# Tile 105 by rows, the first types one group later, the second block's steps six tiles later

## Chip, cores and metric

The kernel runs on one core of a Trainium2 chip. The metric is the device time of one execution in microseconds (us): the median over the runs of a kernel.

## What is computed

A graph layer with relations: 12,500 nodes with 256 features, 212,500 edges that are sorted by their end (`dst`), and a type of 8 for each edge. `h` is the normalised and rectified `x`. Each edge sends its source's `h` through the weight of its type; a node sums what comes in, and adds a bias, its own `h` through a loop weight, and `x`.

```python
h   = maximum(layernorm(x), 0)                # 12500 x 256
hx  = einsum('ni,rio->rno', h, weight)        # 8 types
msg = hx[edge_type, src]                      # 212500 x 256
agg = segment_sum(msg, dst, num_segments=12500)
out = x + sqrt(0.5) * agg + h_bias + sqrt(0.5) * (h @ loop_weight)
```

## The kernel before

**Turned about.** The kernel sums the `h` rows of the edges by (end node, type) first and multiplies by the weights afterwards. The sums stand in a ring in SBUF (`acc`, 768 columns of nodes for each of 8 types and two halves of features).

**Tiles and units.** The edges are cut into 1578 tiles, two to a unit. One tile is at most 128 source rows, fetched into a buffer `msg` (one row to a partition). `edge_sums(t)` (line 1019) multiplies them on PE with one-hot columns that DVE makes (`onehots`, L1001), into one of four PSUM banks; `add_sums(u)` adds a unit's bank to the ring on DVE (L1072). The first units form block 0 (80 units, tiles 0 to 159), then come blocks of 128 units; for each block `prepare(b)` is a list of small steps, most of them on DVE, that work out its source indices (`gidx`), the columns of its one-hots, the last edge of each node and the places in the ring.

**Fetching rows.** Nearly every tile is fetched by one indirect transfer that POOL issues (`gather`, L944). The first 88 tiles take raw rows of `x` and are normalised in place; later ones take rows of `h`, which the kernel writes to DRAM in its first part (rows loaded and stored by SP, L894 and L900; normalisation is queued to the end at tile 28). A ring of 66 buffers holds tiles; `goal(t)` says how far gathers may run ahead: 64 tiles, from tile 170 on falling to 24, and less at the very end. Each gather also waits in the program for the unit last summed when it is issued.

**Single tiles by rows.** From tile 155 on, every 26th tile (155, 181, ..., 55 in all) is not gathered: `single_rows(t)` is true for it, and `begin_fetch` puts four pieces of 32 rows into queues of SP and ACT, two pieces each. A piece loads 32 offsets into registers (`load_sources`, L965) and issues 32 transfers of one row (L973, 1 KB). `fetch` takes up to four entries of each queue at each tile, from HOLD = 8 tiles after the tile would have been gathered. PE waits on a counter for the 128 rows (L1036) ahead of that tile's sums.

**Groups.** 98 groups of 128 nodes (the first has 84) follow in order: when a group's last unit is summed, its 18 products (L1252) are spread between the tiles' sums, then `finish(g)` adds bias and `x` and hands over the store. `finish(g)` also readies the ring's slot of group g + 6: for the first eight groups the slot is only cleared on ACT (`clear`); from group 8 on `begin(b)` writes each node's own edge into it, a transpose of its rows of `h` on PE and eight DVE operations (L1114). For that, the types of those own edges must be known, for four groups at a time (index q): `mark(q)` (DVE, L1135) and `find_types(q)` (a product on PE, L1145; comparisons on DVE, L1152 and L1157; a product that spreads them, L1164; a cast, L1168). The first q that needs this is `plan.typed` = 2, groups 8 to 11.

**One bank for odd jobs.** Transposes and products of this kind share the PSUM bank `pt`. `shared` queues such a job, `advance` starts the first one that is ready, and keeps ROOM = 5 tiles between them; where a product needs a result that is still queued, the queue is forced through in order (`advance(None)`).

**Order.** The program is written out by the Python loop `for t in range(NT)`; each engine then works through its own list in that order. Steps of a block have a due tile, start of the block's list + LOADED (EARLY for block 1) + number, and run about one a tile when a budget (`credit`) allows. Before, block 1's 46 steps start at tile 31 and end at tile 93; group 0 is finished at tile 55, group 1 at 69, group 2 at 87, group 3 at 103, group 4 at 121.

Of the kernel before, what the change touches and what calls it, by code (L numbers as in the profile page):

```python
# [20 lines left out]
SP = mybir.EngineType.SP  # L21
ACT = mybir.EngineType.Activation
# [6 lines left out]
XG = 4  # L29
# [12 lines left out]
NEAR = 8  # L42
# [13 lines left out]
AHEAD = 64  # L56
# [5 lines left out]
CLOSE = 8  # L62

SINGLE = 26
FETCH = 4
SOURCES = 32
BY_SP = (0, 2)
# [7 lines left out]
QUAD = 4  # L75
# [18 lines left out]
LATE = -4  # L94
# [1 line left out]

PREP = 232
LOADED = 20
EARLY = 30
HELD = 30  # L100
SETTLE = 4
ROOM = 5
# [149 lines left out]
def kernel(  # L252
# [20 lines left out]
    plan = Plan(N, E)  # L273

    NT = plan.NT
# [13 lines left out]
    h32 = dram.tile([N, D], F32, name="h32")  # L289
# [41 lines left out]
    with ExitStack() as main:  # L331
# [37 lines left out]
        state = {"h32": None}  # L369
# [439 lines left out]
        for d in range(0, N, XG * P):  # L809
            k = min(XG, (N - d) // P)  # L810
# [101 lines left out]

        def single_rows(t):

            return (t % SINGLE == SINGLE - 1 and t + 2 * NEAR < NT
                    and state["h32"] is not None and t // QUAD * QUAD >= state["h32"] + LATE + AHEAD)

        def begin_fetch(t):

            if t not in msg:  # L920
                room(t - t % PAIR)
            fetched[t] = len(fetched)
            for k, r in enumerate(range(0, P, SOURCES)):
                engine = SP if k in BY_SP else ACT
                fetches[engine].append((
                    done["tile"] + HOLD,
                    lambda r=r, engine=engine: load_sources(t, r, engine)))
# [177 lines left out]
        def begin(g):  # L1105

            s0, n = slot(g)
            q = g // XG
            o = plan.starts[g] - plan.starts[XG * q]
            turn, keep, pst = turn_nodes(g, selves)  # L1110

            def own(r):
                of = typed[q][:, o : o + n].unsqueeze(1).to_broadcast([P, KC, n])
                i = nc.vector.scalar_tensor_tensor(  # L1114
                    acc[:, :, r, s0 : s0 + n], of, float(r + 1), pst[:, :, :n],
                    op0=ALU.is_equal, op1=ALU.mult)
                in_run("own", i, r == R - 1)
                if r == R - 1:
                    zeroed[g, "slot"] = i.ins

            def write():
                for r in range(R):
                    writes.append((g, 0.42, lambda r=r: own(r)))

            shared(turn, [(2, write), (2, keep)], lambda: q in typed)
# [101 lines left out]
        def group_work(g):  # L1227

            d0 = plan.starts[g]
            s0, n = slot(g)  # L1230
            first_dep = [True]
            final = plan.NG - 1 if plan.NG > SLOTS + 1 else None

            def biased(g):
                q, k = divmod(g, XG)
                n = plan.ends[g] - plan.starts[g]
                rows_ = got["x", q]
                nc.vector.tensor_add(rows_[:n, k, :], rows_[:n, k, :], outs[g % 2][:n, 1, :])  # L1238

            def product(r, c, g=g):  # L1240
                n = plan.ends[g] - plan.starts[g]
                if (r, c) == (R, 0):
                    while g == final and final - 2 not in finished:
                        late.pop(0)[1]()
                    got["out", g] = outs[g % 2][:, 0, :]
                if r == R:
                    while ("self", g) not in got:
                        advance(None)
                    lhs, rhs = got["self", g][:, c, :n], wl[:, c, :]
                else:  # L1250
                    lhs, rhs = acc[:, c, r, s0 : s0 + n], w[:, c, r * D : (r + 1) * D]
                i = nc.tensor.matmul(got["out", g][:n], lhs, rhs, start=(r == R and c == 0),  # L1252
                                     stop=(r == R - 1 and c == KC - 1))
                latest["pe"] = in_run(
                    "loops" if r == R else "products", i, r >= R - 1 and c == KC - 1).ins
                if (r, c) == (R, 0) and g < 2:
                    tc.add_manual_dep(i.ins, done["bias"], SYNC_DEP, reason="one engine at a time")
                if r < R and first_dep[0]:
                    first_dep[0] = False
                    tc.add_manual_dep(i.ins, added[plan.last[g]].name, SYNC_DEP, reason="sums complete")  # L1260

            def finish():
                finished.add(g)
                q, k = divmod(g, XG)
                rows_ = got["x", q]
                if g != final:
                    biased(g)
                nc.vector.tensor_add(rows_[:n, k, :], rows_[:n, k, :], got["out", g][:n])  # L1268
                if final is not None and g != final and done["tile"] >= NT - HELD:
                    alone = rows_[:n, k, :]  # L1270
                    stores.append((NT, lambda: nc.sync.dma_start(out[d0 : d0 + n], alone)))
                elif XG * (q + 2) >= plan.NG or n < P:
                    nc.sync.dma_start(out[d0 : d0 + n], rows_[:n, k, :])
                elif k == XG - 1:
                    first = plan.starts[XG * q + shorts(q)]
                    to, of = out[first : d0 + n].rearrange("(k p) d -> p k d", p=P), rows_[:, shorts(q) :, :]
                    stores.append((done["tile"] + STORE, lambda: nc.sync.dma_start(to, of)))
                b = g + SLOTS
                q, k = divmod(b, XG)
                if b < plan.NG:  # L1280
                    if q < plan.typed:
                        clear(b)
                    else:
                        begin(b)
                if q + 1 >= plan.typed and XG * (q + 1) < plan.NG:
                    if k == max(XG // 4, SLOTS - XG * q):
                        load_groups("h", h32, q + 1)
                    if k == XG - 2 + (q + 1 == plan.typed):
                        mark(q + 1)
                    if k == XG - 1:  # L1290
                        find_types(q + 1)

            def last():
                done["late"].append((done["tile"] + REST, finish))

            work = []
            for r in [R, *range(R)] if g != final else range(R):
                for c in range(KC):
                    work.append((0.55, lambda r=r, c=c: product(r, c)))
            work.append((0.0, last))  # L1300
            if final is not None and g == final - 1:
                work = [(0.55, lambda c=c: product(R, c, final)) for c in range(KC)] + work
                work.append((0.0, lambda: biased(final)))
            return work
# [290 lines left out]
```

## Time and profile before

| | us |
|---|---|
| median of 3 runs | 1935.35 (1934.03 to 1936.07) |
| profiled execution | 1935.85 |
| span in that profile | 1934.1 |
| PE busy | 1683.9 (87%) |
| POOL busy | 1448.6 (75%) |
| DVE busy | 1313.7 (68%) |
| ACT busy | 132.0 (7%) |

The span runs from the first to the last instruction; the execution's own time has 1.75 us more. PE is TensorE, DVE VectorE, ACT ScalarE, POOL GpSimd, SP SyncE. An engine's busy time doesn't count the issuing of transfers by SP and ACT, register loads, or waits. A row of a timeline gives start, duration, engine, line, operation and tiles, and in brackets the idle time ahead of it with what ended it; SPq is SP issuing transfers.

### The profile page before, as it was taken

The page shows a single profiled execution, that of the slowest core. Times are in us where ns is not written, and L with a number is a line of the kernel's source. Part 1 is how long each engine was busy: PE and PEld are TensorE (multiplying, and loading weights), DVE is VectorE, ACT ScalarE, POOL GpSimd, SP SyncE. Part 2 cuts the span into 40 slices and gives each one's busy share as a digit, 9 for nine tenths or more (in the row PEclk, how much of TensorE's full clock was granted, in tenths as well). Part 3 has the DMA queues.
Part 4 walks back from the last instruction along what each step waited for, and adds up shares of the span by engine and source line. Part 5 has one row for each costly group of instructions (what it writes and reads, how often), then busy time and mean ns, then how long its engine had stood idle before and what let it go on. Part 6 is the DMA issues. An engine that isn't in the chain of part 4 may idle for free.

```text
span 1934.1 us, 41835 instructions
## 1 busy us (share of the span) xinstructions
PE 1683.9 (87%) x10152; PEld 1477.3 (76%) x10152; DVE 1313.7 (68%) x3304; ACT 132.0 (7%) x286; POOL 1448.6 (75%) x1549
## 2 busy tenths in 40 slices
PE   2367999998998898989898898989998898889998
PEld 2357889897897777878787776777777688777987
DVE  6878768975776865667776666776566685665662
ACT  6964000000000000000000000000000000000000
POOL 7777777777777777777777777777777777777774
PEclk9568999999999998998999999999999999999999
DMA  9974445544454444454444454444444445444443
GB/s 315 381 225 138 133 129 142 142 133 133 131 143 133 132 131 134 131 142 133 132 133 133 132 141 134 131 132 132 131 123 122 133 131 143 121 139 131 112 117 93
DMA packets 159789, 279.23 MB, mean 144 GB/s; under 512 B 36319, under 2 KB 110802, under 8 KB 159538
## 3 DMA queue, kind: packets, MB, share of 16 engines
q0 software_dynamic: 73104, 199.72, 36.6%
q1 hardware_dynamic: 77384, 73.17, 12.5%
q10 hardware_dynamic: 9050, 3.63, 1.1%
q8 instruction: 80, 1.31, 0.3%
q14 instruction: 171, 1.40, 0.2%
HBM read 250.78 MB, written 25.60 MB: 143 GB/s over the span
## 4 chain that ended last, share of the span: by engine, by line
PE 36%; DMA 29%; POOL 13%; issue 7%; DVE 6%; SPq 6%; ACT 2%; DVEq 0%; POOLq 0%; ACTq 0%; PEldq 0%
DMA msg<-h,gidx 26%; PE po L1252 18%; PE ps L1039 17%; POOL msg L944 13%; SPq L973 5%; DVE acc L1072 1%; SPq L965 1%; ACT msg L876 1%; DMA msg<-h 1%; DVE stats L832 1%; DMA xt<-in_x_dram 1%; DVE oh L1001 1%; DVE moves L458 1%; ACT xt L876 0%; DVE acc L1114 0%
## 5 line engine op out<-in xcount | busy, mean ns | idle before, releaser
L944 POOL DMA_INDIRECT msg<-h,gidx x1435 | 1362.6, 950 | 438.7 <-issue 368.2
L1039 PEld LDWEIGHTS ps<-oh,msg 128*128 128x128 f32 x6312 | 942.4, 199 | 349.0 <-DMA msg<-h,gidx 204.1
L1039 PE MATMUL ps<-oh,msg 128*128 128x136 f32 (+1 forms) x6312 | 995.6, 289 | 202.6 <-DMA msg<-h,gidx 121.4
L1252 PE MATMUL po<-w,acc 128*128 128x256 f32 (+1 forms) x3136 | 892.5, 390 | 2.0 <-DVE acc L1072 1.7
L1072 DVE TENSOR_TENSOR acc<-acc,ps 128x352 f32 x789 | 408.4, 518 | 372.3 <-PE ps L1039 364.4
L1252 PEld LDWEIGHTS po<-w,acc 128*128 128x128 f32 (+1 forms) x3136 | 521.8, 194 | 41.7 <-issue 12.4
L1114 DVE SCALAR_TENSOR_TENSOR acc<-types,pt 128x256 f32<-128x256 bf16 x720 | 259.7, 414 | 71.7 <-PE pt L1096 64.2
L1001 DVE TENSOR_TENSOR oh<-fixed,cols 128x544 f32<-128x544 f32 x395 | 282.8, 716 | 0.0
L1252 PE MATMUL po<-wl,self_t 128*128 128x256 f32 (+1 forms) x392 | 117.7, 427 | 8.5 <-DVE self_t L1101 6.1
L944 POOL DMA_INDIRECT msg<-in_x_dram,gidx x86 | 82.0, 953 | 26.9 <-issue 23.8
L1252 PEld LDWEIGHTS po<-wl,self_t 128*128 128x128 f32 (+1 forms) x392 | 74.6, 212 | 18.9 <-DVE self_t L1101 7.5
L1168 DVE CAST types<-pt 128x512 bf16<-128x512 f32 x23 | 15.9, 691 | 54.2 <-PE pt L1164 54.2
L1238 DVE TENSOR_TENSOR xr<-xr,po 128x256 f32<-128x256 f32 (+1 forms) x98 | 40.6, 414 | 15.8 <-PE po L1252 15.8
L1268 DVE TENSOR_TENSOR xr<-xr,po 128x256 f32<-128x256 f32 (+1 forms) x98 | 41.2, 421 | 10.6 <-PE po L1252 7.3
L876 ACT ACTIVATE msg<-msg,shift,rstd 128x256 f32<-128x256 f32 x88 | 44.8, 587 | 7.1 <-DVE stats L840 5.3
L1101 DVE COPY self_t<-pt 128x256 f32<-128x256 f32 (+1 forms) x98 | 40.8, 417 | 3.3 <-PE pt L1096 2.8
L458 DVE TENSOR_SCALAR moves<-fixed 128x271 int32<-128x271 int32 (+1 forms) x90 | 40.6, 451 | 3.4 <-DVE acc L1072 2.2
L1096 PE MATMUL pt<-ident,hr 128*128 128x128 f32 (+1 forms) x196 | 38.8, 281 | 2.2 <-DMA hr<-h 1.0
L460 DVE COPY_PREDICATED fixed<-moves,fixed 128x311 int32<-128x311 int32 (+14 forms) x90 | 38.0, 422 | 3.1
L876 ACT ACTIVATE xt<-xt,shift,rstd 128x256 f32<-128x256 f32 x66 | 33.7, 587 | 10.3 <-DVE shift L873 10.3
L1152 DVE TENSOR_TENSOR of<-pt,line 22x512 bf16<-22x512 f32 x23 | 15.7, 682 | 25.3 <-PE pt L1145 25.1
L1096 PEld LDWEIGHTS pt<-ident,hr 128*128 128x128 f32 (+1 forms) x196 | 25.7, 150 | 4.4 <-DVE types L1168 1.6
(167 smaller groups left out, 367.5 us busy)
## 6 DMA issues: line engine op xcount, KB each, us to landing
msg<-h SPq DMA_DIRECT2D x3520, 1.0 KB
msg<-h ACTq DMA_DIRECT2D x3520, 1.0 KB
msg<-h,gidx POOLq DMA_INDIRECT x1435
hr<-h SPq DMA_DIRECT2D x23, 512.0 KB
xr<-in_x_dram SPq DMA_DIRECT2D x23, 512.0 KB
out_dram<-xr SPq DMA_DIRECT2D x22, 512.0 KB
xt<-in_x_dram SPq DMA_DIRECT2D x16, 512.0 KB
h<-xt SPq DMA_DIRECT2D x16, 512.0 KB
```

The costliest lines, as they stand in the source:

```text
L458: nc.vector.tensor_single_scalar(m, packed[:, :n], 1 << (bit + k), op=ALU.bitwise_and)
L876: nc.scalar.activation(row, row, AF.Relu, bias=shift[:n, j : j + 1], scale=rstd[:n, j : j + 1])
L944: i = nc.gpsimd.indirect_dma_start(out=msg[t], out_offset=None, in_=table[:, :], in_offset=bass.IndirectOffsetOnAxis(ap=of, axis=0))
L973: j = queue.dma_start(msg[t][r0 + i : r0 + i + 1, :].bitcast(U8), h32_bytes[:, bass.ds(v, D * 4)])
L1001: j = nc.vector.tensor_tensor(o[:, k : k + v, :i, :width], iota_f[:, :width].unsqueeze(1).unsqueeze(1).to_broadcast([P, v, i, width]), of. ...
L1039: j = nc.tensor.matmul(ps[:, c, first : first + width], m[:, c * P : (c + 1) * P], o[:, :width], start=(i == 0 and c == 0), stop=(end and ...
L1072: i = nc.vector.tensor_tensor(a, a, ps, op=ALU.add)
L1096: in_run("turns", nc.tensor.transpose(pst[:, c, :n], rows_[:n, c * P : (c + 1) * P], ident[:n, :n]), c == KC - 1)
L1101: nc.vector.tensor_copy(got["self", g][:, :, :n], pst[:, :, :n])
L1114: i = nc.vector.scalar_tensor_tensor(acc[:, :, r, s0 : s0 + n], of, float(r + 1), pst[:, :, :n], op0=ALU.is_equal, op1=ALU.mult)
L1252: i = nc.tensor.matmul(got["out", g][:n], lhs, rhs, start=(r == R and c == 0), stop=(r == R - 1 and c == KC - 1))
L1268: nc.vector.tensor_add(rows_[:n, k, :], rows_[:n, k, :], got["out", g][:n])
```

## The change

Three edits. Tile 105 joins the tiles that are fetched row by row, and for it alone all four pieces go to SP's queue. The marks and types for q = 2 move from `finish(1)` to `finish(2)`, where group 8 begins (behind the call of `begin(8)`, whose job waits for the types); later q keep their places. Block 1's steps come due six tiles later.

```diff
+ALONE = 105
...
-EARLY = 30
+EARLY = 36
...
         def single_rows(t):
 
-            return (t % SINGLE == SINGLE - 1 and t + 2 * NEAR < NT
-                    and state["h32"] is not None and t // QUAD * QUAD >= state["h32"] + LATE + AHEAD)
+            return ((t == ALONE or t % SINGLE == SINGLE - 1) and t + 2 * NEAR < NT
+                    and state["h32"] is not None
+                    and (t == ALONE or t // QUAD * QUAD >= state["h32"] + LATE + AHEAD))
...
             for k, r in enumerate(range(0, P, SOURCES)):
-                engine = SP if k in BY_SP else ACT
+                engine = SP if k in BY_SP or t == ALONE else ACT
...
                     else:
                         begin(b)
+                        if b == XG * plan.typed:
+                            mark(q)
+                            find_types(q)
                 if q + 1 >= plan.typed and XG * (q + 1) < plan.NG:
                     if k == max(XG // 4, SLOTS - XG * q):
                         load_groups("h", h32, q + 1)
-                    if k == XG - 2 + (q + 1 == plan.typed):
+                    if k == XG - 2 and q >= plan.typed:
                         mark(q + 1)
-                    if k == XG - 1:
+                    if k == XG - 1 and q >= plan.typed:
                         find_types(q + 1)
```

Here q and k belong to group b = g + 6, whose slot `finish(g)` readies.

## The prediction

> **What bounds the kernel now.** I read the page first (busy shares, costliest groups), then who waited for whom on POOL, then POOL's timeline.
>
> ```profile
> span 1934.1 us, 41835 instructions
> ...
> PE 1683.9 (87%) x10152; PEld 1477.3 (76%) x10152; DVE 1313.7 (68%) x3304; ACT 132.0 (7%) x286; POOL 1448.6 (75%) x1549
> ...
> L944 POOL DMA_INDIRECT msg<-h,gidx x1435 | 1362.6, 950 | 438.7 <-issue 368.2
> L944 POOL DMA_INDIRECT msg<-in_x_dram,gidx x86 | 82.0, 953 | 26.9 <-issue 23.8
> ```
>
> ```profile
> POOL msg L944 <- issue: 392.3, 1286, 0.3
> POOL msg L944 <- PE ps L1039: 57.4, 183, 1.2
> ```
>
> PE has the larger busy share, so it looks like the bound. The two lines on waits say otherwise: in front of nearly every gather POOL is idle for 0.3 us (392.3/1286, 57.4/183), "issue" being no wait at all. A gather thus costs 0.95 + 0.30 = 1.25 us of POOL whether anyone is late or not, and POOL's 75% is a saturated engine. The next rows are from POOL's timeline, and a window of 200 us (its fifth count is POOL's gathers).
>
> ```profile
> 3.73 1.11 POOL L944 DMA_INDIRECT msg<-in_x_dram,direct  x1 [1.11 <-DMA direct<-in_src_dram]
> ...
> 34.82 0.94 POOL L944 DMA_INDIRECT msg<-in_x_dram,gidx  x1 [1.02 <-PE ps L1039]
> ...
> 176.53 0.99 POOL L944 DMA_INDIRECT msg<-h,gidx  x1 [1.16 <-PE ps L1039]
> ...
> 1915.31 0.94 POOL L944 DMA_INDIRECT msg<-h,gidx  x1 [0.30 <-issue]
> ```
>
> ```profile
> 1000.00:1200.00 200.00, 179.55 (x1091) 152.98 (x1092) 124.09 (x283) 0.00 (x0) 151.34 (x160) 0.98 0.49 137
> ```
>
> There are 1435 + 86 gathers and the 2 of the first unit, 1523 in all; from the first start to the last, (1915.31 - 3.73)/1522 = 1.256 us each; in steady state 200/160 = 1.25. So the stream of gathers runs from 3.7 to 1916.3 us practically without a hole. Holes from a wait are two: at 34.82 (1.02 instead of 0.30; the change leaves what it waits for as it is) and at 176.53 (1.16 instead of 0.30, so 0.86 us lost). Whatever takes a gather away, or fills such a hole, moves everything behind it; whatever PE or DVE gain elsewhere moves nothing. The end hangs on that stream by a fixed tail, shown by the chain of waits:
>
> ```profile
> 1885.30 3.85 DMA msg<-h,gidx
> ...
> 1929.02 0.42 DVE xr L1268
> ```
>
> The last wait for a gather ends at 1885.30 + 3.85 = 1889.2; then PE works through to the end. An earlier stream brings that point and the end forward by the same.
>
> **Tile 105 by rows.** One gather of 1523 goes: -1.25 us for every gather behind tile 104, if POOL finds no new wait. In its place SP issues 128 row transfers of 1 KB and four register loads. Rows for their cost and for what SP does at that time, from SP's timeline, the chain of waits (one register load) and PE's timeline:
>
> ```profile
> 116.41 0.38 SPq L1189 DMA_DIRECT2D hr<-h  x1
> ...
> 147.53 0.35 SPq L1273 DMA_DIRECT2D out_dram<-xr  x1
> ...
> 148.99 0.51 SPq L1189 DMA_DIRECT2D hr<-h  x1
> ...
> 192.48 6.14 SPq L973 DMA_DIRECT2D msg<-h  x19
> ```
>
> ```profile
> 383.57 2.34 SPq L965
> ```
>
> ```profile
> 121.64 2.52 PE L1039 MATMUL ps<-oh,msg 128*128 128x104 f32 x10 [4.84 <-DVE acc L1072]
> ...
> 206.90 1.13 PE L1252 MATMUL po<-wl,self_t 128*128 128x256 f32 x4 [0.52 <-DVE self_t L1101]
> ...
> 209.19 0.59 PE L1039 MATMUL ps<-oh,msg 128*128 128x104 f32 x4
> ```
>
> A row costs 6.14/19 = 0.32 us of SP, a register load about 2.3. Tile 105 comes up for gathering at tile 42, so the fetch starts at 42 + HOLD = 50 and, at four entries a tile, its 132 entries fill tiles 50 to 82. The first row must wait until PE has used the old content of the buffer (tiles 38 and 39, in the row at 121.64, so by 124.2). Until group 0 is finished (tile 55) that is one load and 23 rows, 2.3 + 7.4 = 9.7 us, done near 134, in a stretch where SP idles (116.8 to 147.5). Then SP stands at group 0's store, as before, until 147.5; behind it remain 105 x 0.32 + 3 x 2.3 = 40.5 us of rows and the three loads of groups that stand between them (1.5 us): done near 190. PE comes to tile 105 at 209.2, and rows of tile 155, for which SP was waiting till 192.48, find it free. The loads now behind rows (second block of x and h, issued by 149.5 before) come some 10 us later; their first reader, the turn of group 4, comes right before the product at 206.90. So this part costs nothing on the path; cover about 15 us; without it PE stands at tile 105, and POOL with it once the ring of 66 buffers is used up.
>
> **First marks and types.** Working through the order that the Python loop writes out, group 1 finishes at tile 69, group 2 at tile 87. Before, marks and the product that finds types stood at tile 69:
>
> ```profile
> 159.28 1.96 PE L1039 MATMUL ps<-oh,msg 128*128 128x136 f32 x16
> ...
> 170.70 1.01 PE L1145 MATMUL pt<-mark,loops 128*54 128x512 bf16 x2 [9.46 <-DVE mark L1135]
> ...
> 173.51 0.96 PE L1039 MATMUL ps<-oh,msg 128*128 128x136 f32 x4
> ...
> 175.17 0.59 PE L1039 MATMUL ps<-oh,msg 128*128 128x104 f32 x4
> ...
> 169.77 0.48 DVE L1135 TENSOR_SCALAR mark<-line,firsts 128x512 bf16<-128x512 f32 x1
> ...
> 171.75 0.68 DVE L1152 TENSOR_TENSOR of<-pt,line 22x512 bf16<-22x512 f32 x1
> ```
>
> PE is through with tile 69 at 161.2 and DVE, behind, makes the two marks (0.48 each) from 169.77; PE in its order cannot pass the product (L1145) and stands 9.46 us. Tiles 70 and 71 (173.51 and 175.17) are done late, and theirs are the buffers that POOL needs for the gather of tile 136 (136 = 70 + 66): that is the hole at 176.53. This matters twice. With the marks left at tile 69, the 1.25 us of the first part would be eaten here, since POOL would only come sooner to the same wait. With the marks gone, PE goes on and the hole's 0.86 us comes back too.
>
> What is late next? (a) At tile 87 the product now waits for DVE's marks. From 185 us on it is DVE that waits for PE:
>
> ```profile
> 186.74 0.42 DVE L1101 COPY self_t<-pt 128x256 f32<-128x256 f32 x1 [0.57 <-PE pt L1096]
> ...
> 192.71 0.42 DVE L434 COPY cols<-pt 128x256 f32<-128x256 f32 x1 [1.48 <-PE pt L430]
> ...
> 191.86 0.59 PE L1039 MATMUL ps<-oh,msg 128*128 128x104 f32 x4
> ...
> 199.12 0.95 POOL L944 DMA_INDIRECT msg<-h,gidx  x1 [0.30 <-issue]
> ...
> 199.57 1.08 DVE L1114 SCALAR_TENSOR_TENSOR acc<-types,pt 128x256 f32<-128x256 bf16 x3
> ...
> 204.83 0.42 DVE L1101 COPY self_t<-pt 128x256 f32<-128x256 f32 x1
> ...
> 217.88 0.95 POOL L944 DMA_INDIRECT msg<-h,gidx  x1 [0.30 <-PE ps L1039]
> ```
>
> So DVE's backlog is gone at tile 87 (about 189 us) and PE loses there between 0 and, as at tile 69, 9.46 us; but what it loses it had kept since tile 69, as DVE's work up to tile 87 is the same but for the comparison (0.68, L1152) and the two like it that now follow. I take PE at tile 88 1 to 2 us earlier than before. Slack there: tile 89 is done at 192.4 and the gather that takes its buffers (tile 154) starts at 199.12: 6.7 us, less the 0.8 that lay between the end of tile 71 (175.76) and the gather at 176.53, and less the 2.1 by which POOL comes sooner, leaves 4. Queued behind the product on PE are group 3's products and tiles 88 onward.
>
> (b) Types are now known 14 to 25 tiles later (the one PSUM bank for such jobs takes one each 7 tiles: product at 87, columns of block 1 at 94, spread at 101). The start of group 8's slot (begin(8), eight L1114, 1.08/3 = 0.36 us each, and a copy of 0.42), before at tile 96, will not have run by tile 103, where group 4's first product forces the queue through: PE waits 8 x 0.36 + 0.42 = 3.3 us more there. Tile 105 is done at 209.8, its buffers are taken by the gather at 217.88: 8.1 us, less 0.8 as above, less 2.1, less 3.3, plus the 1.5 of (a): 3.4 us left. Costs nothing, but this is the thinnest cover. Group 8's slot must be clear at tile 113; it is.
>
> **Steps from tile 36.** All 46 steps of block 1 on DVE come six tiles later, none is added. Their deadlines (indices at tile 96, column numbers at 154, places at 128) are over 10 tiles behind; block 1 is listed near tile 75, ahead of the marks at 87, so none is forced. Cost nothing; gain only that DVE has six steps less to do ahead of tile 69. Which gathers a DVE operation lengthens can change:
>
> ```profile
> 111.09 1.24 POOL L944 DMA_INDIRECT msg<-in_x_dram,gidx  x1 [0.30 <-issue]
> ...
> 115.28 1.28 POOL L944 DMA_INDIRECT msg<-h,gidx  x1 [0.30 <-issue]
> ...
> 111.03 0.47 DVE L476 TENSOR_TENSOR rise<-nat_d 128x312 f32<-128x312 int32 x1
> ```
>
> Both gathers start just after such a step does and last 0.3 us longer than 0.95: with the moved steps this falls differently. If all such hits of the first steps went, the 0.29 + 0.33 = 0.6 us of these two came back; as much may be lost to new ones; I take 0. The Trainium skill (SBUF — State Buffer, section "SBUF: two separate sides") has a VectorE operation that takes the shared port lock GpSimd out of writing descriptors, and a 620 ns transfer growing to 3100; by that estimate each hit costs 2.5 us, and two hits more than before would turn the sum into a loss of 2.9. The trace has hits, but of 0.3 us.
>
> **Sum.** -1.25 - 0.86 = -2.1 us. The profiled execution took 1935.85, 1.75 outside its span of 1934.1: span 1932.0, execution 1933.7. It stands 0.5 above the median of the runs, 1935.35, so the median goes to 1933.2, 0.11% less. A measurement of this kernel tells about 0.2%, 3.9 us, from no change: this is within it.
>
> **Rivals.** (1) The gain is eaten: POOL finds a hole of about 2 us behind the chain at tile 103 or the product at 87. For it: 3 to 4 us of cover, worked out from several durations. Against: POOL loses only what exceeds the cover. Time 1935.3. (2) Slower: the product at tile 87 waits 9.46 us, as at tile 69, while PE kept nothing of the earlier stall, because DVE is the bound all through. Then 9.46 + 1.0 - 4 = 6.5 us of POOL are lost: 1933.2 + 6.5 = 1939.7. It decides once PE reaches tile 88 over 4 us later than before. Against it: the DVE rows at 186.74 and 192.71, which wait for PE. (3) Tile 105 late: were a row to cost 0.65 us instead of 0.32, SP would end near 225 and POOL lose some 8 us; the row at 192.48 is half of that. (4) Faster by over 3.9 us: POOL's own rate would have to change, for which no row speaks. That the change does nothing would need tile 105 to stay a gather; the condition holds at tile 42, since normalisation ended at tile 28.
>
> **How the numbers follow.** Forecast 0.72 (own range 1932.2 to 1934.3, from the 0.6 of lengthened gathers and the spread of the runs), rival 1 0.13, rivals 2 and 3 together 0.09, rival 4 0.06. Range 1931.8 to 1936.6: it takes in the forecast and rival 1, and leaves out the slow cases and rival 4. Faster by over 0.2%: 0.07 (rival 4 and an edge of the forecast); slower 0.10 (rivals 2 and 3, and an edge of rival 1); same 0.83.
>
> **What would show it.** Right: 1434 + 86 + 2 gathers, no idle over 0.3 us on POOL near 175, last gather starting near 1913.2, no PE wait of 9 us ahead of L1145 at 161, all rows of tile 105 from SP between 122 and 195. Wrong: a POOL idle of over 1 us between 185 and 220, PE standing at the row counter (L1036) near 205, or a last gather not 2 us earlier with an unchanged tail.

## The result and the profile after

The changed kernel took 1940.05 us (median of 13 runs, 1938.08 to 1943.92), the kernel before, measured beside it, 1935.05 us (13 runs, 1934.03 to 1937.95): ratio 1.0027, 95% interval 1.0019 to 1.0034. It is slower by 5 us, where 2 us less were forecast, and lies above the range. The profiled execution took 1943.53 us, 3.5 above its median, with a span of 1941.7. In what follows lines of the changed kernel stand two or three higher than before (a gather is L946, sums are L1041).

The page of the changed kernel:

```profile
span 1941.7 us, 42094 instructions
...
PE 1683.8 (87%) x10152; PEld 1479.4 (76%) x10152; DVE 1314.7 (68%) x3304; ACT 132.0 (7%) x286; POOL 1447.7 (75%) x1548
...
L946 POOL DMA_INDIRECT msg<-h,gidx x1434 | 1362.3, 950 | 447.6 <-issue 372.7
...
L946 POOL DMA_INDIRECT msg<-in_x_dram,gidx x86 | 81.3, 946 | 26.9 <-issue 23.5
```

One gather is gone (1434 for 1435) and no engine's work has grown; POOL's idle time ahead of the `h` gathers went from 438.7 to 447.6. POOL's timeline shows where (all rows from 100 us on with over 0.35 us of idle time, and the last gather):

```profile
198.39 0.94 POOL L946 DMA_INDIRECT msg<-h,gidx  x1 [1.07 <-PE ps L1041]
...
219.50 0.94 POOL L946 DMA_INDIRECT msg<-h,gidx  x1 [3.89 <-PE ps L1041]
...
486.54 0.94 POOL L946 DMA_INDIRECT msg<-h,gidx  x1 [2.42 <-PE ps L1041]
...
490.91 0.94 POOL L946 DMA_INDIRECT msg<-h,gidx  x1 [3.43 <-PE ps L1041]
...
497.66 0.94 POOL L946 DMA_INDIRECT msg<-h,gidx  x1 [0.81 <-issue]
...
1923.38 0.95 POOL L946 DMA_INDIRECT msg<-h,gidx  x1 [0.30 <-issue]
```

The hole at 176.5 is gone, as forecast. In its place are two at 198 and 219 (0.77 + 3.59 us beyond the 0.30 of every gather) and three from 486 to 498 (2.12 + 3.13 + 0.51). Together 10.1, less 1.25 for the gather, 0.86 for the old hole and 0.5 for a tail that was 0.5 shorter: 7.5, and the spans differ by 7.6. The sum by holes closes; what is left to explain is why PE freed buffers late at 198 and 219, and again at 486. PE's timeline of the changed kernel:

```profile
190.14 1.01 PE L1147 MATMUL pt<-mark,loops 128*54 128x512 bf16 x2 [2.65 <-DVE mark L1137]
191.09 2.07 PE L1254 MATMUL po<-wl,self_t 128*128 128x256 f32 x4
...
195.33 0.59 PE L1041 MATMUL ps<-oh,msg 128*128 128x104 f32 x4
...
211.68 0.44 PE L431 MATMUL pt<-ident,col 128*128 128x128 f32 x2 [2.62 <-DVE self_t L1103]
212.63 0.69 PE L1098 MATMUL pt<-ident,hr 128*128 128x128 f32 x2 [0.52 <-DVE cols L435]
213.84 2.08 PE L1254 MATMUL po<-wl,self_t 128*128 128x256 f32 x4 [0.52 <-DVE self_t L1103]
...
218.32 0.90 PE L1041 MATMUL ps<-oh,msg 128*128 128x104 f32 x4
...
485.09 1.18 PE L1041 MATMUL ps<-oh,msg 128*128 128x104 f32 x4 [7.80 <-PEq L1038]
```

The product that finds types waits 2.65 us at tile 87; the queue forced through at tile 103 waits 2.62 + 0.52 + 0.52. Tile 89, 192.4 before, ends at 195.9; tile 105, 209.8 before, at 219.2. And around these waits, from 184.8 and from 212.1 us on, PE works at half pace. Windows of both kernels (length; busy us of PE, PEld, DVE, ACT, POOL with counts; granted clock, DMA share, GB/s), the changed one first:

```profile
185.00:195.00 10.00, 7.35 (x23) 5.84 (x24) 7.80 (x18) 0.00 (x0) 7.67 (x8) 0.50 0.38 108
...
212.00:219.00 7.00, 5.97 (x20) 4.74 (x19) 3.03 (x9) 0.00 (x0) 2.84 (x3) 0.51 0.34 85
```

```profile
185.00:195.00 10.00, 10.00 (x71) 9.47 (x70) 6.57 (x18) 0.00 (x0) 7.56 (x9) 1.00 0.38 108
...
212.00:219.00 7.00, 7.00 (x49) 6.59 (x49) 6.13 (x15) 0.00 (x0) 5.29 (x6) 1.00 0.44 115
```

In both windows the granted clock was 0.50 and 0.51 in place of 1.00, and PE got 23 and 20 matmuls done where it had done 71 and 49. Group 3's first products and the tiles between them, 16 matmuls from 191.09 to 195.92, took 4.8 us; the same from 189.65 to 192.45 before, 2.8 (the row below, and the one at 191.86 in the prediction).

```profile
189.65 1.05 PE L1252 MATMUL po<-wl,self_t 128*128 128x256 f32 x4
...
473.92 1.18 PE L1039 MATMUL ps<-oh,msg 128*128 128x104 f32 x4 [7.13 <-PEq L1036]
```

The Trainium skill (TensorE: Matmul & The Clock Gate, Part 1: the HAM clock gate) has the array fall to half rate after an idle window of about 3.4 us and come back after one that is busy. The trace agrees in the rate and in the length (the stretches of the changed kernel last 10.2 and 6.8 us, three and two times 3.4). No one idle window stands ahead of the first drop: from 170 to 184.7 us PE was busy 10.7 of 14.7 us, with no wait over 1.5 us, so here many short waits were enough. The Trainium skill has such a case too (TensorE: Matmul & The Clock Gate, Part 1, "A second HAM failure mode"): frequent short idles between groups of matmuls make the clock swing.

### The profile page after: what moved, and what is told of

The parts are those of the page before. It is cut to its first block, busy times and chain, and to the rows that moved or that the text cites. A ratio compares the mean times of both kernels' runs of the same rounds, so it can differ in the third digit from the quotient of the medians.

```text
span 1941.7 us, 42094 instructions
## 1 busy us (share of the span) xinstructions
PE 1683.8 (87%) x10152; PEld 1479.4 (76%) x10152; DVE 1314.7 (68%) x3304; ACT 132.0 (7%) x286; POOL 1447.7 (75%) x1548
## 4 chain that ended last, share of the span: by engine, by line
PE 34%; DMA 27%; POOL 14%; DVE 8%; issue 8%; SPq 6%; ACT 2%; DVEq 0%; POOLq 0%; PEldq 0%; ACTq 0%
DMA msg<-h,gidx 23%; PE po L1254 18%; PE ps L1041 15%; POOL msg L946 14%; SPq L975 5%; DMA msg<-h 2%; DVE acc L1074 2%; DVE oh L1003 1%; SPq L967 1%; DVE acc L1116 1%; DVE moves L459 1%; ACT msg L877 1%; DVE stats L833 1%; DMA h<-xt 1%; DMA xt<-in_x_dram 1%
## 5 line engine op out<-in xcount | busy, mean ns | idle before, releaser
L946 POOL DMA_INDIRECT msg<-h,gidx x1434 | 1362.3, 950 | 447.6 <-issue 372.7
L1041 PEld LDWEIGHTS ps<-oh,msg 128*128 128x128 f32 x6312 | 945.1, 200 | 350.0 <-DMA msg<-h,gidx 206.4
L1041 PE MATMUL ps<-oh,msg 128*128 128x136 f32 (+1 forms) x6312 | 996.6, 289 | 206.7 <-DMA msg<-h,gidx 128.9
L1254 PEld LDWEIGHTS po<-w,acc 128*128 128x128 f32 (+1 forms) x3136 | 520.6, 194 | 47.2 <-DVE acc L1074 11.6
L946 POOL DMA_INDIRECT msg<-in_x_dram,gidx x86 | 81.3, 946 | 26.9 <-issue 23.5
```

What stands on the lines that cost most here:

```text
L946: i = nc.gpsimd.indirect_dma_start(out=msg[t], out_offset=None, in_=table[:, :], in_offset=bass.IndirectOffsetOnAxis(ap=of, axis=0))
L1041: j = nc.tensor.matmul(ps[:, c, first : first + width], m[:, c * P : (c + 1) * P], o[:, :width], start=(i == 0 and c == 0), stop=(end and ...
```

## The experiments

My theory after the result (T): PE is late at 198 and 219 because DVE holds it behind the moved steps and marks, and each wait is made dearer by the halved clock; GpSimd then finds no free buffer. Rivals: tile 105's rows on SP (B), the steps or the marks alone, the clock as first cause, or chance of one execution. Ratios are always against the kernel before on the same chip, since chips differ (it took 1935 to 1936 us in three of the sets of runs, 1940.03 on the chip of the first four experiments). In the expectations of these four, theory A is that the types come too late whatever the steps do, B that the rows on SP are the cause, C that the moved steps are.

**Tile 105 by rows alone.**

```diff
+ALONE = 105   (with the rows on SyncE; marks and EARLY = 30 as before)
```

> Of the change only tile 105 by rows from SP; marks at group 1's finish and steps from tile 31, as before. Theory A (the types come too late, PE loses 7 us and more at tiles 87 to 105, and POOL and the later row tiles pay): none of that here; the hole in front of POOL's gather of tile 136 grows from 1.16 to about 2.4 us and eats the saved gather, no POOL hole near 219 or 490; time of before, 1935 +- 1. Theory B (the 128 rows on SP are the cause): POOL holes near 219 and 490 stay, 1940 or more. Theory C (the steps from tile 36 are the cause): as A.

Measured: 1940.38 us (11 runs, as in the next three), ratio 1.0005 (0.9996 to 1.0014). From POOL's timeline, its one hole behind 100 us:

```profile
176.42 0.95 POOL L946 DMA_INDIRECT msg<-h,gidx  x1 [2.25 <-PE ps L1041]
```

The hole of 1.16 grew to 2.25: the gather that was saved is eaten by the wait behind the marks at tile 69, as the prediction said of this part alone. No hole at 198, 219 or 490. B as the whole cause falls.

**The marks alone, at the third group's result; then marks and steps without tile 105.**

```diff
 marks_only:   EARLY = 30, marks and types for q = 2 in finish(2)
 marks_steps:  EARLY = 36, marks and types for q = 2 in finish(2)
```

> Of the change only the marks and types at group 2's finish; steps from tile 31, tile 105 gathered. Theory A: the hole at tile 136 (0.86 us) goes, but PE waits for the marks at tile 87 and for the queue at tile 103, POOL holes of 0.5 to 4 us between 195 and 222 and more near 490: 1937 to 1944. Theories B and C: hole at 136 gone and nothing else, 1934.2.

> The change without tile 105 by rows. Theory A: all of the change's holes, and the gather that was saved is back: 1.25 us above the changed kernel's 1940, at most less what POOL now comes later to its holes; 1940 to 1942. Theory B: no hole at 219 or 490, 1934.2. Theory C: 1940 to 1942, as A, but marks_only stays at 1934.2.

Measured: marks alone 1937.8 us, ratio 0.9993 (0.9984 to 1.0002), and no hole from 100 us on; with the steps 1940.46, ratio 1.0004 (0.9995 to 1.0013), and in POOL's timeline

```profile
219.02 0.95 POOL L944 DMA_INDIRECT msg<-h,gidx  x1 [3.24 <-PE ps L1039]
```

So the steps, to which I had given no cost, are what makes the difference between the two: 2.7 us between medians, and a hole of 2.9 us beyond the 0.30. That is theory C by the holes, but not by the time: 5 to 7 us above the kernel before were expected of marks and steps together, and it was 0.4 (-1.0 to 2.5). The profile of the marks alone is of their fastest run (1932.93 us); most of the 4.9 us to its median would be the length of its gathers, a median of 946 ns against 949 in the other three profiles of that chip, 4.6 us over 1523 (an estimate). Where the steps went is seen in windows of DVE's work (third busy time): the kernel before, the marks alone, the change.

```profile
120.00:140.00 20.00, 13.48 (x69) 11.37 (x70) 18.38 (x54) 13.23 (x37) 15.13 (x17) 0.67 0.59 169
140.00:160.00 20.00, 19.39 (x126) 17.51 (x126) 18.31 (x56) 16.88 (x46) 15.13 (x17) 1.00 0.62 188
160.00:175.00 15.00, 5.54 (x25) 4.23 (x25) 13.96 (x50) 8.33 (x19) 11.34 (x13) 0.66 0.37 105
```

```profile
120.00:140.00 20.00, 13.65 (x67) 11.53 (x67) 17.94 (x51) 13.40 (x37) 15.22 (x16) 0.65 0.60 176
140.00:160.00 20.00, 19.48 (x127) 17.58 (x126) 18.74 (x57) 16.60 (x44) 15.33 (x16) 1.00 0.62 189
```

```profile
120.00:140.00 20.00, 15.98 (x85) 13.47 (x86) 17.02 (x51) 15.05 (x43) 15.13 (x16) 0.74 0.60 175
140.00:160.00 20.00, 17.87 (x118) 16.34 (x116) 16.57 (x52) 15.12 (x40) 15.13 (x16) 1.00 0.53 142
160.00:175.00 15.00, 10.73 (x63) 9.08 (x64) 14.38 (x41) 8.27 (x19) 11.34 (x12) 1.00 0.55 173
175.00:190.00 15.00, 8.91 (x50) 7.79 (x49) 14.18 (x58) 2.37 (x5) 11.46 (x12) 0.83 0.39 110
```

From 120 to 160 us DVE did 36.7 us of work in the first two and 33.6 in the third. The missing 3.1 us are put off past 160, where DVE is busy 28.6 of 30 us and PE 19.6: there DVE is the bound, and the marks reach it late. From the end of tile 71 to that of tile 87 PE took 23.5 us in the change and 19.0 with the marks alone. With the marks alone tile 89 ends at 187.7, nearly 5 us ahead of the kernel before; with steps and marks at 195.5. DVE's timeline in the change shows the last of that backlog, without idle time before the marks:

```profile
189.20 0.48 DVE L1137 TENSOR_SCALAR mark<-line,firsts 128x512 bf16<-128x512 f32 x1
...
191.19 0.68 DVE L1154 TENSOR_TENSOR of<-pt,line 22x512 bf16<-22x512 f32 x1 [0.68 <-PE pt L1147]
```

The backlog is only a part of it: the moved steps also change the order in the one bank for odd jobs. DVE's and PE's timelines with the marks alone:

```profile
185.76 0.48 DVE L1135 TENSOR_SCALAR mark<-line,firsts 128x512 bf16<-128x512 f32 x1
...
183.84 0.38 PE L430 MATMUL pt<-ident,col 128*128 128x128 f32 x2
...
190.80 0.61 PE L1145 MATMUL pt<-mark,loops 128*54 128x512 bf16 x2
...
204.78 0.27 PE L731 MATMUL pt<-ident,pos 128*1 128x128 f32 x1 [3.17 <-DVE self_t L1101]
```

There block 1's columns are ready first and take the bank behind tile 85; the product that finds types comes behind tile 92, 4 us after the marks, and waits for nothing. At tile 87, which ended at 185.1, it too would have waited, for the second mark is done at 186.7. In the change the columns are not ready when the bank comes free: the product stands right behind tile 87 and waits, and the columns are forced through at tile 103. Of the 8.2 us by which tile 89 ends later in the change than with the marks alone, 2.4 are there at the end of tile 87; the other 5.8 are the wait, the product and the halved clock behind it. The steps thus cost by way of DVE's backlog and of the bank's order; no run moves one without the other.

The marks alone do pay at tile 103 (3.17 us in the last row, and a clock that is halved from 205.7 to 212.5), but from a lead of 5 us: tile 105 ends at 212.0, 2.2 later than before, and no hole follows.

**The change with tile 363 gathered.**

```diff
-            return ((t == ALONE or t % SINGLE == SINGLE - 1) and t + 2 * NEAR < NT
+            return (t != 363 and (t == ALONE or t % SINGLE == SINGLE - 1) and t + 2 * NEAR < NT
```

> The changed kernel with tile 363 gathered instead of fetched by rows (one gather more, 1.25 us). Theory A with the late rows of tile 363 as the second link: PE's wait of 7.8 us ahead of tile 363 and POOL's three holes near 490 (5.5 us together in the profile) go, the holes at 198 and 219 (4.4 us) stay; profile near 1939, median 1936 to 1938. If PE's delay alone made the holes near 490, without the rows, they stay: 1941.

Measured: 1941.6 us, ratio 1.0007 (0.9998 to 1.0016). The holes from 486 to 498 are gone. That at 198, which was to stay, is gone as well, and one is left before:

```profile
217.07 0.95 POOL L946 DMA_INDIRECT msg<-h,gidx  x1 [2.57 <-PE ps L1041]
```

So the holes near 490, 5.8 of the change's 10.1 us of holes, hang on tile 363's rows: PE stood 7.80 us at their counter and started at 485.09, where it stood 7.13 before and started at 473.92. In nine profiles there are holes near 490 in the three where PE starts tile 363 at 483.7 or later (the change, and two below), and in none of the six where it starts (or would have) at 476.5 or earlier. Two delays come together: PE is 9 to 10 us behind at tiles 105 to 155, and SP's 128 rows more shift its queue (its rows for tile 363 start at 427.1 before, 430.1 with tile 105's rows alone, 431.8 with marks and steps alone, 438.7 with all three). Singly they make 2.9 and 4.6 us of the 11.6, so part of this shift is not explained.

Up to tile 363's rows this run is the same program as the change. Its clock was halved for 3.4 us at tile 87, from 189.1 on, in place of 10.2, and tile 89 ended at 193.6: how long the clock stays down differs between executions. The hole between 217 and 220 stands in all four profiles in which the columns are forced at tile 103 (the change, marks with steps, this one and the next) and in none of the other five on chips of this pace.

**TensorE kept busy.** Three fp32 matmuls more in each even tile from 70 to 86, into columns that nothing reads, else the change.

```diff
+            if i == 0 and 70 <= t < 88:
+                for _ in range(3):
+                    nc.tensor.matmul(bank[:, 384:512], ident, ident, start=False, stop=False, ...)
```

> Three fp32 matmuls more in each even tile from 70 to 86 into unused columns (27 in all), else the change. Theory T with the clock as the cause: no half-clock stretch at 185 to 195, tile 89's sums end near 193 in place of 196, no hole at 198, that at 219 at 1.5 us or less. Rival (DVE's work alone holds TensorE, the clock costs nothing): tile 89 at 196 or later, both holes as in the changed kernel or larger.

Measured: 1944.57 us (4 runs), ratio 1.0044 (1.0027 to 1.0061). A row of PE's timeline, the window 185 to 195, and POOL's timeline:

```profile
189.09 0.59 PE L1151 MATMUL pt<-mark,loops 128*54 128x512 bf16 x2 [3.12 <-DVE mark L1141]
```

```profile
185.00:195.00 10.00, 6.88 (x32) 5.72 (x32) 7.27 (x17) 0.00 (x0) 7.56 (x9) 0.83 0.37 107
```

```profile
217.73 0.94 POOL L946 DMA_INDIRECT msg<-h,gidx  x1 [3.26 <-PE ps L1041]
...
491.12 0.94 POOL L946 DMA_INDIRECT msg<-h,gidx  x1 [4.63 <-PE ps L1041]
```

The clock stayed up until the product, which waited all the same (3.12 us, for DVE) and the clock fell right behind it, for 3.4 us. From tile 87 to 89 PE took 8.2 us, 8.4 in the change, and tile 89 ended at 194.2, later than the 193 expected; of its 1.7 us ahead of the change, 1.3 were there at tile 69 already. The hole at 198 went; the one at 219 hardly shrank. What the extra matmuls did is not shown by this, since the change with tile 363 gathered had neither them nor the early drop nor the hole at 198. Both runs say the same of the clock as first cause: with full clock up to the product, the product still waits over 3 us for DVE and the hole near 218 stays. DVE's lateness comes first, the clock raises its price.

**Group 8's turn later,** so that it isn't forced through at tile 103; else the change.

```diff
-                        begin(b)
+                        if b == XG * plan.typed:
+                            later[done["tile"] + 17] = lambda: begin(b)
+                        else:
+                            begin(b)
...
+                later.pop(t, lambda: None)()
```

> The change with group 8's turn called 17 tiles later, so that it isn't forced through at tile 103. Theory T: the waits at tile 103 shrink by 1 to 2 us, the half-clock stretch at 212 to 219 goes or moves, the hole at 219 falls to 0.5 us or less, that at 198 stays. Rival (TensorE is late from tiles 70 to 89 alone): the hole at 219 stays above 2.5 us.

Measured: 1937.97 us (11 runs, 1934.07 to 1943.01), ratio 1.0011 (1.0002 to 1.0020), 0.0016 or 3 us below the change's, measured on another chip. PE's and POOL's timelines:

```profile
209.78 1.13 PE L1254 MATMUL po<-wl,self_t 128*128 128x256 f32 x4 [0.52 <-DVE self_t L1103]
...
229.32 0.60 PE L1098 MATMUL pt<-ident,hr 128*128 128x128 f32 x2 [1.97 <-DVE offs L736]
```

```profile
198.38 0.94 POOL L946 DMA_INDIRECT msg<-h,gidx  x1 [1.26 <-PE ps L1041]
...
485.12 0.94 POOL L946 DMA_INDIRECT msg<-h,gidx  x1 [3.73 <-PE ps L1041]
...
490.23 0.94 POOL L946 DMA_INDIRECT msg<-h,gidx  x1 [4.16 <-PE ps L1041]
```

As T expected: one wait of 0.52 at tile 103 in place of three (3.1 us less, where 1 to 2 were expected), full clock from 212 to 219, the hole at 219 gone, that at 198 kept. The lost time comes back on PE at 229 (1.97 us, then a half-clock stretch), where POOL doesn't feel it, but tile 155 ends at 266.7, 267.3 in the change, and so tile 363 is late again in this profile, which was of the slowest of the 11 runs.

**A version with an earlier search.** The kernel before with tile 105's rows, marks where they stood before, the search let into the queue at tile 73, less room between jobs, steps from tile 30.

```diff
+ALONE = 105
+SHY = 4
...
-            shared(find, [(2, kinds_of)])
+            shared(find, [(2, kinds_of)], wait=SHY if q == plan.typed else 0)
...
-                        done["free"] = done["tile"] + ROOM
+                        done["free"] = done["tile"] + (4 if done["tile"] < 110 else ROOM)
```

> The kernel before with tile 105's rows by SyncE and the marks at the end of the second group's steps, the search given 4 tiles of waiting (tile 73), the room between shared jobs 4 tiles up to tile 110, steps from tile 30. Theory T: no holes at 176, 198 or 219 above 1 us and one gather less, so about 2 us below the kernel before. Rival (any hurry of the chain holds TensorE at tiles 70 to 90): a half-clock stretch between 185 and 220 us with a hole of over 1 us behind it, time the same or above the kernel before.

Measured: 1933.91 us (11 runs), ratio 0.9987 (0.9978 to 0.9996): faster than the kernel before, and by the ratios than the change, which ran on another chip. The page, PE's timeline, and from POOL's timeline one hole and the last gather:

```profile
span 1933.2 us, 42098 instructions
```

```profile
171.13 0.59 PE L1148 MATMUL pt<-mark,loops 128*54 128x512 bf16 x2 [1.17 <-DVE mark L1138]
```

```profile
1903.12 0.94 POOL L947 DMA_INDIRECT msg<-h,gidx  x1 [1.19 <-PE ps L1042]
...
1914.35 0.94 POOL L947 DMA_INDIRECT msg<-h,gidx  x1 [0.30 <-issue]
```

The search waits 1.17 us in place of 9.46, tile 89 ends at 191.6 and tile 105 at 209.0, and POOL's timeline has no idle over 0.33 us from 100 to 1900. The median is 1.8 us below that of the kernel before, close to the 2 us that were forecast for the change: less the gather, less the hole. In the profile the span is only 0.9 shorter, with a hole of 0.9 beyond the 0.30 near the end (1903.12). As the marks' place and the bank's room differ from the change too, this doesn't show that the steps alone stood in the way; the change with steps at tile 30 was not run.

**On three other chips** everything took some 2500 us. There the change and the last three kernels had been run first:

> The changed kernel once more, so that the three others of this call have it on their own chip. Theory T (TensorE is late: DVE holds it at tiles 70 to 87, its clock is then halved from 185 to 195 and from 212 to 219 us, and GpSimd, 28 us ahead of nothing, runs out of copied tiles): 3 to 7 us above the kernel before, holes of about 1 us near 198 and 3 to 4 us near 219; the holes near 490, which hang on single rows landing late, in part of the runs. Rival (the holes are chance of one execution): within 1 us of the kernel before, holes elsewhere or none.

> The change, with three extra fp32 matmuls into unused columns of the bank in each even tile from 70 to 86 (27 in all; the result doesn't use them). They fill TensorE's waits for DVE there and take nothing away. Theory T with the clock as the cause: no half-clock stretch at 185 to 195, tile 89's sums end near 193 in place of 196, the hole at 198 is gone and that at 219 is 1.5 us or less, time 2 to 4 us below the changed kernel's. Rival (only DVE's total work holds TensorE, the clock drop costs nothing): tile 89 at 196 or later, holes at 198 and 219 as in the changed kernel or larger, time the same or up to 5 us worse.

> The change, with group 8's turn (the first step of the second block's third stack) called 17 tiles later, so that it is no longer forced through at tile 103 together with the columns and the fourth turn. Theory T: the 3.3 us of chained waits at tile 103 shrink to about 2, the half-clock stretch at 212 to 219 goes or moves to after tile 113, the hole at 219 falls from 3.6 us of excess to 0.5 or less, the hole at 198 stays (0.8 us); time 2 to 3 us below the changed kernel's. Rival (TensorE is late from tiles 70 to 89 alone, whatever is forced at 103): the hole at 219 stays above 2.5 us and the time within 1 us of the changed kernel's.

> The kernel before with tile 105's rows fetched by SyncE, the marks at the end of the second group's steps with the search for types allowed 4 tiles of waiting, the room between shared jobs 4 tiles in place of 5 up to tile 110, and steps still from tile 30: the search is placed at tile 73 and the columns at 90, early enough that nothing but the fourth turn and its placing is forced at tile 103. Theory T: no holes at 176, 198 or 219 above 1 us, one gather less, so 1.25 + 0.86 = about 2 us below the kernel before. Rival (any further hurry of the chain holds TensorE at tiles 70 to 90): a half-clock stretch of 6.8 us or more between 185 and 220 us with a hole of over 1 us behind it, time the same or above the kernel before.

Then the same on the second and, without the change, on the third of these chips:

> The changed kernel on another chip than that of the last four runs, where SyncE issued its rows at 0.5 to 0.8 us each in place of 0.32 and GpSimd was not the bound. Theory T (DVE holds TensorE at tiles 70 to 87, its clock is then halved near 185 to 195 and 212 to 219 us, and the next rows of GpSimd run out of free tiles): 3 to 7 us above the kernel before, holes near 198 (about 1 us) and 219 (3 to 4 us), those near 490 in part of the runs. Rival (chance of one execution): within 1 us of the kernel before, no hole above 1 us between 190 and 225.

> Three fp32 matmuls more in each even tile from 70 to 86 into unused columns (27 in all), else the change. Theory T with the clock as the cause: no half-clock stretch at 185 to 195, tile 89's sums end near 193 in place of 196, no hole at 198, that at 219 at 1.5 us or less, time 2 to 4 us below the changed kernel's on the same chip. Rival (DVE's work alone holds TensorE, the clock costs nothing): tile 89 at 196 or later, both holes as in the changed kernel or larger, time the same or up to 5 us worse.

> The change with group 8's turn called 17 tiles later, so that it isn't forced through at tile 103. Theory T: the waits at tile 103 take about 2 us in place of 3.3 beyond the kernel before's, the half-clock stretch at 212 to 219 goes or moves, the hole at 219 falls to 0.5 us or less, that at 198 stays; 2 to 3 us below the changed kernel on the same chip. Rival (TensorE is late from tiles 70 to 89 alone): the hole at 219 stays above 2.5 us, time within 1 us of the changed kernel's.

> The kernel before with tile 105's rows by SyncE and the marks at the end of the second group's steps, the search given 4 tiles of waiting (tile 73), the room between shared jobs 4 tiles up to tile 110, steps from tile 30. Theory T: no holes at 176, 198 or 219 above 1 us and one gather less, so 1.25 + 0.86 = about 2 us below the kernel before. Rival (any hurry of the chain holds TensorE at tiles 70 to 90): a half-clock stretch between 185 and 220 us with a hole of over 1 us behind it, time the same or above the kernel before.

> Three fp32 matmuls more in each even tile from 70 to 86 into unused columns (27 in all), else the change. Theory T with the clock as the cause: no half-clock stretch at 185 to 195, tile 89's sums end near 193 in place of 196, no hole at 198, that at 219 at 1.5 us or less. Rival (DVE's work alone holds TensorE, the clock costs nothing): tile 89 at 196 or later, both holes as in the changed kernel or larger.

> The change with group 8's turn called 17 tiles later, so that it isn't forced through at tile 103. Theory T: the waits at tile 103 shrink by 1 to 2 us, the half-clock stretch at 212 to 219 goes or moves, the hole at 219 falls to 0.5 us or less, that at 198 stays. Rival (TensorE is late from tiles 70 to 89 alone): the hole at 219 stays above 2.5 us.

> The kernel before with tile 105's rows by SyncE and the marks at the end of the second group's steps, the search given 4 tiles of waiting (tile 73), the room between shared jobs 4 tiles up to tile 110, steps from tile 30. Theory T: no holes at 176, 198 or 219 above 1 us and one gather less, so about 2 us below the kernel before. Rival (any hurry of the chain holds TensorE at tiles 70 to 90): a half-clock stretch between 185 and 220 us with a hole of over 1 us behind it, time the same or above the kernel before.

Measured, by chip (the kernel before took 2495.81, 2487.05 and 2489.8 us): the change 1.0049 (1.0014 to 1.0085) and 1.0064 (1.0035 to 1.0092); TensorE kept busy 1.0033 (0.9997 to 1.0069), 1.0047 (1.0022 to 1.0072), 1.0015 (0.9988 to 1.0041); group 8 later 1.0036 (1.0004 to 1.0069), 1.0052 (1.0027 to 1.0078), 1.0058 (1.0022 to 1.0094); the earlier search 1.0014 (0.9977 to 1.0051), 1.0033 (0.9996 to 1.0071), 1.0015 (0.9984 to 1.0047). The first run of the change there, its page and SP's timeline, and SP's timeline of the change on its first chip:

```profile
span 2511.4 us, 42094 instructions
...
L946 POOL DMA_INDIRECT msg<-h,gidx x1434 | 1364.2, 951 | 990.6 <-PE ps L1041 344.9
```

```profile
399.62 4.70 SPq L975 DMA_DIRECT2D msg<-h  x10
```

```profile
299.85 9.24 SPq L975 DMA_DIRECT2D msg<-h  x29
```

A gather takes as long as ever (951 ns), but SP needs 0.47 us for a row there and 0.32 on the first chip, and POOL stands idle for 990.6 us: another bound, so these runs say nothing on the holes at 198, 219 and 490. The times that were expected were missed, the change is slower there too, and why SP is slower wasn't found.

## Why the prediction was wrong

**POOL's saturation, the tail, the sum by holes: right.** They account for 7.5 of 7.6 us of span.

**Tile 105: right alone, free no longer with the rest.** Its rows were issued from 121.5 to 190.2 and PE didn't wait for them; the gain is eaten with the marks at tile 69, as said. Not seen, for I had followed SP only up to tile 155: 128 rows more in its queue are still felt at tile 363 (3 us there), and with PE late they help to open the holes near 490. "Costs nothing on the path" is thus the second step that failed: marks and steps without these rows have no hole there, and in the change 5.8 of 10.1 us of holes are of that place.

**The hole at 176: right,** gone in every kernel in which the marks leave tile 69 or the search waits less.

**Steps from tile 36, "cost nothing": this is the step that failed.** I looked at the steps' deadlines and at DVE ahead of tile 69, and counted fewer steps there as a gain. But DVE had had them to fill its time from 120 to 160; the 3.1 us it did less there were put off to the 30 us behind, where it is the bound. And "none is forced" was wrong: the columns of block 1, reckoned for tile 94, were forced through at tile 103. That the product that finds types stands at tile 87 at all was reckoned rightly, but it is itself the steps' doing and got no price: with steps at tile 30 the columns go first, and the product comes behind tile 92, where it waits for nothing. Marks with steps against the marks alone showed what the steps cost: a hole of 2.9 us at 219, and 2.7 us between medians.

**"DVE's backlog is gone at tile 87", "PE at tile 88 1 to 2 us earlier than before": wrong for the same reasons.** The rows of before in which DVE waits for PE, at 186.74 and 192.71, show a DVE that had caught up while PE stood 9.46 us. Take that stall away and the backlog stays. Tile 89 came 3.4 us later: 2.3 us of lead at tile 87, less a wait of 2.65, about 1 us of the product and 2.0 of halved clock. With the marks alone the sentence would have been too careful (5 us earlier), but because the product then comes behind tile 92.

**The chain at tile 103, 3.3 us: right in kind and nearly in size.** Group 8's start held PE for 2.62 us, and the columns, not reckoned there, for 0.52. The waits in all were 3.66 us, 0.89 before, so 2.8 more; but the clock then halved took 2.5 more (213.84 to 219.22, 5.4 us, against 2.9 from 206.90 before). A granted clock of 0.66 between 160 and 175 us stood in the windows of before, behind the 9.46 us, and was in no term of the sum.

Put into the sum: cover of 3.4 us with PE 1.8 us behind at tile 105 (3.3 less 1.5); PE was 9.4 behind, 7.6 more, so 4.2 us short; the holes at 198 and 219 are 4.36. Rival 2 named 1939.7 and a DVE that is the bound all through, and the time came out there, but by luck: the wait at tile 87 was 2.65 us, not 9.46, and of the 10.1 us of holes 0.8 follow on it, 3.6 on tile 103 and 5.8 on tile 363. That the holes near 490 come in part of the runs only would fit the spread of the runs (1938.08 to 1943.92) and the median's rise of 5.0 us, less than the profile's 7.7; it was not shown. The lengthened gathers, on which the Trainium skill's page on the SBUF bore in the prediction, moved nothing: all gathers took 1444.6 us by the page before and 1443.6 after, and one of 0.95 us is gone.

## What to carry to other kernels

A stall is also the time in which another engine catches up: when it is removed, that engine's backlog has to be followed to the next place that waits for it. A step with a far deadline is free only if the engine has the same idle time later; look at that engine's busy share in the stage where the step lands, and at the order of any queue that the step shares with others. Price a wait of TensorE with what follows at half clock, not by its length alone.

## What the runs showed of the hardware

In the change the granted TensorE clock was 0.50 for 10.2 us from 184.8 on, behind waits of at most 1.5 us each, and for 6.8 us from 212.1 on, around waits of 2.62, 0.52 and 0.52; beside the waits this cost some 2.0 and 2.5 us. The same instructions had it at half for 3.4 us at the first place in another execution. A gather's median length was 946 ns in some profiles and 949 in others, which over 1522 gathers is 4.6 us. Chips differed in the rate at which SP issues rows (0.32 and 0.47 us).
